# Register loads, bias sums, stores by position and early weight splits in a two-layer expert kernel

## The chip, the cores and the metric

The kernel runs on one core of one Trainium2 chip. The metric is the device time of one execution in microseconds (us), the median of several runs. A profile of one further execution shows each engine: TensorE (PE, its weight loads PEld), VectorE (DVE), ScalarE (ACT), GpSimd (POOL) and SyncE (SP, which only issues transfers here).

## The reference

The input x has 32 sequences of 128 tokens with 512 features (4096 tokens). Two layers follow each other; each adds a residual.

```python
# layer 0, condition: a shared expert and 2 of 8 routed experts for each token
shared = (silu(x @ sw1.T) * (x @ sw3.T)) @ sw2.T              # 512 -> 1024 -> 512
s = sigmoid(x @ router_w.T + cond @ router_t_w.T)             # the second term: one row per sequence
_, idx = top_k(s + router_bias, 2); gates = s[idx] / sum(s[idx])
routed = sum over both of gates * (gelu(x @ rw1[e].T) @ rw2[e].T)   # 512 -> 256 -> 512
h = (shared + routed) / 3
# layer 0, feed-forward: each sequence picks one of 8 experts from its last token
sel = argmax(softmax(gelu(h_last @ Wp1 + bp1) @ Wp2 + bp2))
x = x + h + 0.3 * ((gelu(h @ W1[sel] + b1) @ W2[sel] + b2) @ Wo + bo)
# layer 1, condition: tokens mixed with their predecessor, 16 experts chosen by token id
xk, xr = x + (prev - x) * maa_k, x + (prev - x) * maa_r
slot = place of the token in its expert's list, up to 256 tokens each, else dropped
y = square(relu(expert_in @ w_key)) @ w_value, gathered back by slot
z = sigmoid(xr @ w_recept) * y
# layer 1, feed-forward: a recurrence over 32 steps with gates f, i, c, and an output tanh
c = sigmoid(f) * c + sigmoid(i) * tanh(g) ; h = tanh(z @ wo.T + c @ uo.T + bo) ; x = x + h
```

## The kernel before, in words

A float32 product is made of three matmuls: `split` (L64, L65) cuts each operand into a high part (an ACT cast) and a low part (a DVE subtraction that waits for the cast), and `mm3` (L82) adds high times high, high times low and low times high. So every operand goes through ACT and DVE before TensorE may use it. A scheduler orders the instructions of each engine by the program's order and its own costs; `tc.issue_after(x)` keeps an instruction behind x, and `behind(last_split)` keeps one behind both halves of a split. An engine works its queue in order.

The work runs in these stages; the times are those of the profiled execution.

1. 0 to 305 us: the shared expert for the first 16 sequences, in four groups of four sequences (`shared`, with `up` and `down` for each of eight columns). Between its matmuls `mid0` puts the router for all tokens (`router`, tiles xr, xrhl, rt) and `seq_bias` (tiles pr, ps_tb, tbias), the cond @ router_t_w term; the condition `n + w == 1` in `mid0` holds for two half-columns. Later `hook2` runs the steps of `choose` and `slots`, which sort tokens into blocks and slots on DVE, and loads the routed experts' weights. `fetch` puts raw loads on SP. The copies of expert biases into `bias_d` (L770) stand in the program after stage 2, but depend on nothing, and the scheduler put them at 3.6, 17.5 and 18.1 us on SP.
2. 305 to 547 us: routed blocks of 128 token rows of one expert. For each block, `turn_x` transposes gathered rows (ptx) and splits them into xb; `r_up` makes 12 matmuls (pur) against the expert's up weights and a gelu (ge); `turn_h` transposes the result (pth, split into hbr); `r_down` makes 6 matmuls (por) and stores the rows. In the order of TensorE's queue, block i's pur are followed by ptx of block i + 1, the six por of block i - 1 and pth of block i. The expert of a block is known only at run time: `first_col` loads its column offset into a TensorE register (L663, a queue instruction), and each pur and por has an instruction in front of it that computes its address from that register. There are 64 blocks that always run, and up to seven more that run in pairs under `tc.If` (`maybe`, L702), placed after every sixth block from block 16 on. `used` is their number, loaded by four engines.
3. 548 to 827 us: the shared expert for the other 16 sequences; between them `combine` (L793, L794) sums shared and routed output of finished sequences, which `get_o` fetches (o, shc, xc), and `policy` picks each sequence's expert and sorts sequences by expert, so that position p stands for sequence `seq_i[p]`.
4. 827 to 1431 us: the feed-forward of layer 0, one sequence at a time in that sorted order (`up`, `bend`, `down`, tiles pu, pt, hb, po). `combine` for the last four sequences and `policy` for the last eight (`late`) run between them. `close` ends a pair of sequences (pb, x1), `mix_r` forms xr, `send_k` transposes and stores xk rows to `xk_d` and `send_v` stores the receptance rows (pv) to `v_d`. Both stores go to the row of the sequence, `rows_of`, whose number an engine loads into a register (`seq`, L1048).
5. 1431 to 1810 us: the 16 experts of layer 1, each with eight pieces of weights of 512 KB (`fetch_piece`, `split_piece`: rawD, wD; `use_piece`: phD, poD). `fetch_rows` gathers an expert's rows from `xk_d` by `slot_t`, `turn_rows` transposes and splits them (ptD, xe). The results go to `res_d`.
6. 1810 to 2495 us: the recurrence; each step gathers y from `res_d` by `gat_i`, loads r from `v_d`, and multiplies (ptF, then gates ps_c, ps_i, ps_f, output poF).

Of the kernel before, what the change touches and what calls it, by code (L numbers as in the profile page):

```python
# [20 lines left out]
P = 128  # L21
# [28 lines left out]
def tile_kernel(ctx: ExitStack, tc: tile.TileContext, a: dict, out: bass.AP):  # L50
# [44 lines left out]
    bias_d = dram.tile([E0 * P, 3 * KD], F32, tag="bias", name="bias_d")  # L95
    v_d = dram.tile([N, D], F32, tag="v", name="v_d")
    sh_d = dram.tile([(NG // 2 + 1) * GT, D], F32, tag="sh", name="sh_d")
    o_d = dram.tile([NBLK * P, D], F32, tag="o", name="o_d")
    xk_d = dram.tile([N, D], F32, tag="xk", name="xk_d")
# [31 lines left out]
    seq_i = const.tile([P, NB], I32, name="seq_i")  # L131
    s0_i = const.tile([P, NB], U32, name="s0_i")
# [17 lines left out]
    pad = const.tile([P, 416 // 4], F32, name="pad")  # L150
# [7 lines left out]
    with ExitStack() as sa:  # L158
# [6 lines left out]
        def fetch(src, name):  # L165
            t = raw_p.tile([P, D], F32, tag="raw", name=name)
            nc.sync.dma_start(out=t, in_=src)
            return t

# [35 lines left out]
        def fetch_x(g):  # L205
            if g < NG:
                x_raw[g] = [fetch(a["x"][g][:, k, :], f"xraw_{g}_{k}") for k in range(KD)]
# [68 lines left out]
        with ExitStack() as s0:  # L276
# [32 lines left out]
            fetch_sw(1)  # L309
            ps_acc = s0.enter_context(tc.tile_pool(name="ps_acc0", bufs=4, space=PSUM, **kw))  # L310
# [51 lines left out]
            def seq_bias():  # L362

                ps = ps_r.tile([P, NB, E0], F32, tag="r", name="ps_tb")
                for k in range(KD):
                    pr = rtile([P, NB, E0], f"pr_{k}")
                    nc.vector.tensor_tensor(
                        pr,
                        condT[:, k, :].unsqueeze(2).to_broadcast([P, NB, E0]),
                        rtw[:, k, :].unsqueeze(1).to_broadcast([P, NB, E0]),  # L370
                        ALU.mult,
                    )
                    mm(ps, ones, pr, k == 0, k == KD - 1)
                nc.vector.tensor_copy(tbias, ps)
# [3 lines left out]
            def fetch_r(i):  # L378
                g, k = divmod(i, KD)
                if 0 < g < NG:  # L380
                    xrs[i] = fetch(a["x"][g][:, k, :], f"xr_{g}_{k}")
# [165 lines left out]
            def slots():  # L547
# [28 lines left out]
                yield from invert(slot_t, [hi], [lo], NSLOT // P, "st")  # L576
                zero = rtile([P, D], "zero")
# [15 lines left out]
            def cut(m):  # L593
                return min(NR, KD + (NR - KD) * (m - 1) // 15) if m > 0 else 0

            def mid0(n, w):

                if n < KF:
                    m = 2 * n + w
                    for i in range(cut(m), cut(m + 1)):  # L600
                        router(i)
                    for i in range(cut(m + 1), cut(m + 2)):
                        fetch_r(i)
                    if n + w == 1:
                        seq_bias()
# [3 lines left out]
            def hook2(g, c):  # L609

                if g == 0:
                    next(steps[0], None)
                    return
                if g == 1 or (g == 2 and c < 5):
# [40 lines left out]
        with s1:  # L655
# [9 lines left out]
            def r_up(i, e=None):  # L665
                if e is None:
                    with tc.issue_after(last_up[0]) if last_up else nullcontext():
                        e = first_col(i)
                x = xb.pop(i)
# [30 lines left out]
            def maybe(n):  # L700
                es = [first_col(i) for i in pairs[n]]
                with tc.If(used > pairs[n][0]):  # L702
                    for i, e in zip(pairs[n], es):
                        r_up(i, e)
# [8 lines left out]

            for i in range(NFULL + 1):
                if i < NFULL:
                    r_up(i)
                    if i + 1 < NFULL:
                        turn_x(i + 1, bx, "xb")
                    if i + 3 < NFULL:
                        take(i + 3)  # L720
                if i > 0:
                    stored = r_down(i - 1)
                if i < NFULL:
                    turn_h(i)
                n, step = divmod(i - FIRST, STEP)
                if i == FIRST - 4:
                    engines = (nc.tensor, nc.scalar, nc.vector, nc.sync)
                    used = nc.values_load(
                        used_i[0:1, 0:1], engines=[x.engine for x in engines], min_val=NFULL, max_val=NBLK
                    )  # L730
# [38 lines left out]
        for kind, i in BIAS.items():  # L769
            nc.sync.dma_start(out=bias_d[:, bass.ts(i, KD)], in_=a[kind][:, KD * D :])  # L770
# [42 lines left out]
        def policy(b0, b1, sm, ps_t, room=None):  # L813
# [69 lines left out]
            nc.vector.tensor_scalar(idxw[:, b0:b1], srow, part_f, None, ALU.add)  # L883
            seq = stile([P, nb], "seq")
            by_place(seq, num)
            nc.vector.tensor_copy(seq_i[:, b0:b1], seq)
            for k in range(KD):
                by_place(condS[:, k, b0:b1], condT[:, k, b0:b1])

# [8 lines left out]
        raws, bcol, changed = {}, {}, {}  # L898
# [3 lines left out]
        def fetch_w(i):  # L902
            if i < len(todo):
                kind, b = order[todo[i]]
                raws[i] = wg.tile([P, WROW], F32, tag="raw", name=f"rawB_{i}")
                nc.gpsimd.indirect_dma_start(
# [3 lines left out]
                )  # L910
                if kind == "W1a":
# [94 lines left out]

    with ExitStack() as sb:
# [35 lines left out]
        seqs, end_p = {}, None  # L1043

        def seq(p, queue=nc.sync):

            if (p, queue) not in seqs:
                seqs[p, queue] = queue.value_load(  # L1048
                    seq_i[0:1, p : p + 1], min_val=0, max_val=PARTS[where(p)[0]] - 1
                )  # L1050
            return seqs[p, queue]

        def rows_of(t, p, queue=nc.sync):

            return t[bass.ds((seq(p, queue) + where(p)[0] * PARTS[0]) * P, P), :]
# [5 lines left out]
        def fetch_hid(b):  # L1061
            if b < NB:
                hid_raw[b] = lp.tile([P, KD, P], F32, tag="hid", name=f"hidB_{b}")
                nc.sync.dma_start(out=hid_raw[b].rearrange("p k q -> p (k q)"), in_=by_seq(hid_d, b))
# [65 lines left out]
        def close(c, last=False):  # L1130
# [38 lines left out]
            for j in range(PB):  # L1169
                part = where(c * PB + j)[0]  # L1170
                nc.sync.dma_start(
                    out=x1_d[bass.ds(seq(c * PB + j) + part * PARTS[0], 1)].rearrange("o p k q -> (o p) k q"),
                    in_=x1[:, :, j, 1:],
                )
            xks[c] = xk, dx, x1
            return done, mixed

# [14 lines left out]
        def send_k(b, queue=nc.sync):  # L1192
# [6 lines left out]
            return queue.dma_start(out=rows_of(xk_d, b, queue), in_=rows).ins  # L1199

        def send_v(b):
# [6 lines left out]
            nc.sync.dma_start(out=rows_of(v_d, b), in_=r)  # L1208
# [12 lines left out]
        for b in range(-1, NB + 1):  # L1221
            c, j = divmod(b - 1, PB)
            if b + 1 < NB:
# [3 lines left out]
                fetch_hid(b + 3)  # L1227
            gated = b - 4 if b % 2 == 0 and 0 <= b - 4 < NB - 6 else None
# [11 lines left out]

            late, step = divmod(b - 3, 3)
            if 0 <= late < GB and step == 0:
                get_o(NB - GB + late, cb, 1)
            if 0 <= late < GB and step == 2:
                combine(NB - GB + late, ps_t)
            if late == GB and step == 2:
                policy(PARTS[0], NB, cb, ps_t)
            if b + 1 < NB:
                bend(b + 1, "a")

# [37 lines left out]
        with tc.issue_after(k_done), tc.issue_after(rows_done):  # L1288
            for b in range(NB - 4, NB - 2):
                send_v(b)  # L1290
            mix_r(NB // PB - 1, rTp, "rT")
            for b in range(NB - 2, NB):
                send_v(b)

    sf = ctx.enter_context(ExitStack())
    sw_.close()
    with ExitStack() as sd:
        kw = dict(reuse_waits="tile")  # L1300
        R = dict(side="right", **kw)
        first_p = sf.enter_context(tc.tile_pool(name="first_p", bufs=1, **kw))
        swb = sd.enter_context(ExitStack())
        ewb = swb.enter_context(tc.tile_pool(name="ewb", bufs=4, **kw))
        er = sd.enter_context(tc.tile_pool(name="er", bufs=6, **R))
        ex = sd.enter_context(tc.tile_pool(name="ex", bufs=2, **R))
        ewa = sd.enter_context(tc.tile_pool(name="ewa", bufs=8, **R))
        ep = sd.enter_context(tc.tile_pool(name="ep", bufs=2, **R))
        tq = sd.enter_context(tc.tile_pool(name="tq", bufs=3, **R))
        ps_h = sd.enter_context(tc.tile_pool(name="ps_hD", bufs=3, space=PSUM, **kw))  # L1310
        ps_t = sd.enter_context(tc.tile_pool(name="ps_tD", bufs=2, space=PSUM, **kw))
        ps_o = sd.enter_context(tc.tile_pool(name="ps_oD", bufs=3, space=PSUM, **kw))
# [4 lines left out]
        def fetch_piece(p):  # L1317
            if p < NPC:
                e, i = divmod(p, 8)
                raws[p] = er.tile([P, 1024], F32, tag="raw", name=f"rawD_{p}")  # L1320
                nc.sync.dma_start(out=raws[p], in_=a["w_key"][e, i] if i < 4 else a["w_value"][e, i - 4])

        def split_piece(p):
            if p < NPC:
                raw = raws.pop(p)
                ew = ewb if p % 12 >= 8 and p < NPC - 8 else ewa
# [12 lines left out]

        def turn_rows(e):  # L1340
# [45 lines left out]
        AHEAD, RAW = 8, 6  # L1386
        fetch_rows(0)
        for p in range(RAW):
            fetch_piece(p)
        turn_rows(0)  # L1390
        fetch_rows(1)
        for p in range(AHEAD):
            after = r_done if p < 4 else (k_done, rows_done)
            with tc.issue_after(after[0]), tc.issue_after(after[1]):
                split_piece(p)
            fetch_piece(p + RAW)
        for p in range(NPC):
# [14 lines left out]
            if p == NPC - 9:  # L1412
                swb.close()
                uci = sf.enter_context(tc.tile_pool(name="uci", bufs=1, **kw))
                uc, first_part = {}, {}

                def weight(name, pool, stage, bufs, tag="raw", parts=2, queue=nc.sync, pair=None):
# [5 lines left out]
                    for h in range(parts):  # L1423
                        raw = stage.tile([P, w], F32, tag=tag, bufs=bufs, name=f"raw_{name}{h}")
                        s = bass.ts(h, w)
                        queue.dma_start(out=raw, in_=flat[:, s])
# [8 lines left out]
    with sf:  # L1435
# [17 lines left out]
        def get_y(b):  # L1453
# [7 lines left out]
            nc.sync.dma_start(out=r, in_=v_d[b * P : (b + 1) * P, :])  # L1461
# [136 lines left out]
        for t in range(NB):  # L1598
            cT = cT_next
            v = {}  # L1600
            if t == 0:
# [3 lines left out]
                with tc.issue_after(z_done):  # L1605
# [178 lines left out]
```

## Time and profile before

| | us |
|---|---|
| median of 3 runs (2495.82 to 2498.42) | 2498.41 |
| profiled execution, its own time | 2497.22 |
| its span, first to last instruction | 2495.5 |
| TensorE busy in it | 2434.5 |
| DVE, ACT, POOL busy | 1326.8, 1034.5, 412.3 |
| mean granted TensorE clock | 0.991 |

The profile names an instruction by engine, line and tiles ("PE pur L82": a matmul that writes pur). A row of waits says which instruction waited for which, with the total, the count and the longest. A row of a timeline gives start, duration, and, in brackets, idle time before it and what ended that. "PEldq" and "PEq" are TensorE's instruction queue: register loads, branches, semaphore waits. "x31" is a count. In a table of stretches each engine has its busy time and, in brackets, its number of instructions; then come the granted clock, the share of the transfers and GB/s.

### The profile page before, as it was taken

The numbers are of one execution on the slowest core, as the hardware profiler recorded it, in microseconds if no ns is written. First come the engines' busy times: TensorE is split into PE (matmuls) and PEld (weight loads), VectorE is DVE, ScalarE is ACT, GpSimd is POOL, SyncE is SP. The second block draws the span as 40 slices with busy tenths as digits, with TensorE's granted clock in tenths as the row PEclk, the third lists the DMA queues.
The fourth block names the chain that finished last, engine by engine and source line by source line (L and its number), as shares of the span: only waits on it lengthen the run. The fifth ranks groups of instructions, "written<-read, shape, count | busy, mean of one in ns | idle before, by whom it ended". The sixth has DMA issues, their size and how long they took to land.

```text
span 2495.5 us, 36566 instructions
## 1 busy us (share of the span) xinstructions
PE 2434.5 (98%) x12932; PEld 2060.7 (83%) x12932; DVE 1326.8 (53%) x2265; ACT 1034.5 (41%) x1826; POOL 412.3 (17%) x462
## 2 busy tenths in 40 slices
PE   8999999999999899999999999999999999999996
PEld 5788888888888788888888889999978888888885
DVE  7897644456567344454454486766642333333336
ACT  4444533343224454454454376666532222222214
POOL 1000022221233233322222100000010000000003
PEclk9999999999999999999999999999999999999998
DMA  5545544457564333341342487777431111111017
GB/s 181 168 126 169 187 161 161 163 185 238 183 215 165 115 120 127 102 153 57 118 146 94 152 295 232 222 228 234 155 125 39 38 40 42 43 42 38 26 70 280
DMA packets 193402, 351.62 MB, mean 141 GB/s; under 512 B 37504, under 2 KB 72368, under 8 KB 190144
## 3 DMA queue, kind: packets, MB, share of 16 engines
q1 hardware_dynamic: 142080, 246.51, 29.9%
q0 software_dynamic: 36448, 75.95, 10.3%
q10 hardware_dynamic: 14688, 26.75, 3.0%
q8 instruction: 108, 1.77, 0.3%
q14 instruction: 78, 0.64, 0.1%
HBM read 373.94 MB, written 88.65 MB: 185 GB/s over the span
## 4 chain that ended last, share of the span: by engine, by line
PE 49%; DVE 2%; DMA 1%; ACT 0%; issue 0%; POOL 0%; SPq 0%; POOLq 0%; DVEq 0%; ACTq 0%
PE phD L82 7%; PE ps_c L82 7%; PE ps_f L82 7%; PE ps_i L82 7%; PE poD L82 7%; PE poF L82 3%; PE po L82 3%; PE pb L82 2%; PE pv L82 1%; PE ptF L1481 1%; PE ptC L1488 1%; PE ptD L1348 0%; DMA v_d<-r 0%; DMA rawD<-in_w_value_dram 0%; PE ptB L1196 0%
## 5 line engine op out<-in xcount | busy, mean ns | idle before, releaser
L65 DVE TENSOR_TENSOR wD<-rawD,wD 128x1024 fp32r<-128x1024 f32 x128 | 156.4, 1229 | 80.8 <-ACT wD L64 80.7
L82 PE MATMUL p<-xhl,swu 128*128 128x512 f32 x768 | 188.7, 397 | 6.5 <-ACT xhl L64 6.5
L82 PE MATMUL phD<-xe,wD 128*128 128x256 f32 x1536 | 186.9, 282 | 2.0 <-DVE hf L1367 2.0
L82 PEld LDWEIGHTS phD<-xe,wD 128*128 128x128 f32 x1536 | 186.0, 190 | 3.3 <-issue 2.2
L82 PE MATMUL p<-xhl,kept_u 128*128 128x512 f32 x768 | 184.3, 394 | 0.7 <-DVE kept_u L65 0.7
L82 PE MATMUL poD<-wD,hD 128*128 128x512 f32 x768 | 181.3, 392 | 0.0
L82 PEld LDWEIGHTS p<-xhl,swu 128*128 128x128 f32 x768 | 144.6, 190 | 36.9 <-ACT xhl L64 6.5
L82 PEld LDWEIGHTS p<-xhl,kept_u 128*128 128x128 f32 x768 | 141.9, 188 | 30.0 <-DVE kept_u L65 1.1
L82 PEld LDWEIGHTS poD<-wD,hD 128*128 128x128 f32 x768 | 142.0, 188 | 28.4
L64 ACT CAST wD<-rawD 128x1024 fp32r<-128x1024 f32 x128 | 133.2, 1047 | 55.4 <-PE poD L82 50.1
L281 POOL DMA_INDIRECT xg<-in_x_rows_dram,blk_t x71 | 67.6, 952 | 454.9 <-PE ptx L291 246.4
L1456 POOL DMA_INDIRECT y<-res_d,gat_i x32 | 30.8, 962 | 573.6 <-DVE r L1476 492.1
L82 PE MATMUL pur<-r,xb 128*128 x792 | 111.5, 291 | 7.2 <-issue 4.2
L82 PE MATMUL por<-r,hbr 128*128 x396 | 108.0, 407 | 1.2 <-ACT hbr L64 1.2
L82 PEld LDWEIGHTS pur<-r,xb 128*128 128x128 f32 x792 | 99.7, 192 | 9.0 <-issue 6.9
L65 DVE TENSOR_TENSOR xb<-ptx,xb 128x512 fp32r<-128x512 f32 x68 | 47.0, 691 | 106.4 <-ACT xb L64 104.7
L82 PE MATMUL poF<-z,wo_hl 128*128 128x512 f32 x384 | 96.4, 399 | 0.0
L82 PE MATMUL ps_f<-wf_hl,z 128*128 128x512 f32 x384 | 96.2, 399 | 0.0
L82 PE MATMUL ps_c<-wc_hl,z 128*128 128x512 f32 x384 | 94.7, 396 | 0.7 <-ACT z L64 0.7
L82 PE MATMUL pb<-rT,Wo_hl 128*128 128x256 f32 x768 | 94.7, 281 | 0.3 <-DVE rT L65 0.2
L82 PE MATMUL acc<-swd,as 128*128 128x512 f32 x384 | 95.0, 392 | 0.0
L82 PE MATMUL pv<-w_recept_hl,xr 128*128 128x512 f32 x384 | 93.1, 391 | 0.5 <-ACTq L934 0.4
(1017 smaller groups left out, 4955.6 us busy)
## 6 DMA issues: line engine op xcount, KB each, us to landing
rawD<-in_w_key_dram SPq DMA_DIRECT2D x64, 512.0 KB, 4.3
rawD<-in_w_value_dram SPq DMA_DIRECT2D x64, 512.0 KB, 4.4
swr<-in_sw_dram SPq DMA_DIRECT2D x120, 256.0 KB, 3.2
o_d<-obr SPq DMA_DIRECT2D x66, 256.0 KB, 2.4
xraw<-in_x_dram SPq DMA_DIRECT2D x32, 256.0 KB, 4.2
rraw<-in_rw_dram SPq DMA_DIRECT2D x32, 256.0 KB, 3.0
xc<-in_x_dram SPq DMA_DIRECT2D x32, 256.0 KB, 3.5
hid_d<-o ACTq DMA_DIRECT2D x32, 256.0 KB, 2.2
```

Source lines behind the costliest of these rows:

```text
L64: first = nc.scalar.copy(hi, src).ins
L65: done = nc.vector.tensor_tensor(lo, src, hi.bitcast(F32), ALU.subtract).ins
L82: done = nc.tensor.matmul(ps, lhsT=left(hl, k), rhs=right(hr, k), start=start and k + n == 0, stop=stop and 3 * k + n == last,)
L281: nc.gpsimd.indirect_dma_start(out=xg[i], out_offset=None, in_=a["x_rows"], in_offset=bass.IndirectOffsetOnAxis(ap=blk_t[:, i : i + 1], ax ...
L1456: got = nc.gpsimd.indirect_dma_start(out=y, out_offset=None, in_=res_d, in_offset=bass.IndirectOffsetOnAxis(ap=gat_i[:, b : b + 1], axis=0),)
L1481: nc.tensor.transpose(pt[:, k, :], r[:, bass.ts(k, P)], ident)
L1488: nc.tensor.transpose(pt[:, k, :], c[:, bass.ts(k, P)], ident)
```

## The change

- Start: pieces 0 and 2 of the first group's x are loaded by ACT's queue. Router loads have their own six buffers and stay behind the first loads. `cut` begins the router two half-columns later. `seq_bias` sums its four products on DVE, makes one product on TensorE, and is called once, at the last column of group 0. The three copies into `bias_d` go to group 1's first columns, each behind the last load.
- Routed blocks: `know(i)` loads the register of a block, behind the last pur of the block before it. The registers of conditional blocks are loaded the same way, in the blocks before their branch; `used` is loaded behind a pur as well.
- Stage 4: `get_o`, `combine` and `policy` of the late sequences stand behind named loads and behind bend's split. xk and v rows are stored at the row of the position, without a register. `policy` notes `pos_i` and `moved` (how far a sequence's rows are shifted), and `by_position` corrects `slot_t` with it.
- Layer 1: the pools for raw pieces, rows and five weight pieces are opened early; the first pieces are fetched and five of them split before or amid the last gates of stage 4. One store to `x1_d` goes behind those loads.
- Recurrence: r is loaded from the row of the position, with a register load on SP for each sequence. One weight load is kept behind the last r load.
- The tile pad shrinks from 416 to 32 bytes for three new small tiles.

```diff
-        def fetch(src, name):
+        def fetch(src, name, queue=nc.sync):
...
+                x_raw[g] = [
+                    fetch(a["x"][g][:, k, :], f"xraw_{g}_{k}", nc.scalar if g == 0 and k % 2 == 0 else nc.sync)
+                    for k in range(KD)
+                ]
...
-                    mm(ps, ones, pr, k == 0, k == KD - 1)
+                    if k > 0:
+                        nc.vector.tensor_tensor(pr, pr, sum_, ALU.add)
+                    sum_ = pr
+                ps = ps_r.tile([P, NB, E0], F32, tag="r", name="ps_tb")
+                mm(ps, ones, sum_, True, True)
...
-                return min(NR, KD + (NR - KD) * (m - 1) // 15) if m > 0 else 0
+                return min(NR, KD + (NR - KD) * (m - 3) // 13) if m > 2 else 0
...
-                    if n + w == 1:
-                        seq_bias()
...
+                if g == 1 and c % 2 == 0 and c < 6:
+                    kind = list(BIAS)[c // 2]
+                    with tc.issue_after(last_load[0]):
+                        nc.sync.dma_start(out=bias_d[:, bass.ts(BIAS[kind], KD)], in_=a[kind][:, KD * D :])
...
-            def r_up(i, e=None):
-                if e is None:
+            cols = {}
+
+            def know(i):
+
+                if i < NBLK:
                     with tc.issue_after(last_up[0]) if last_up else nullcontext():
-                        e = first_col(i)
-                x = xb.pop(i)
+                        cols[i] = first_col(i)
+
+            def r_up(i):
+                x, e = xb.pop(i), cols.pop(i)
...
             def maybe(n):
-                es = [first_col(i) for i in pairs[n]]
                 with tc.If(used > pairs[n][0]):
...
+            know(0)
             for i in range(NFULL + 1):
+                n, step = divmod(i - FIRST, STEP)
                 if i < NFULL:
                     r_up(i)
                     if i + 1 < NFULL:
+                        with tc.issue_after(loads[0]) if i == FIRST - 3 else nullcontext():
+                            know(i + 1)
+
+                        if -3 <= i - FIRST and n + 1 < len(pairs) - 1 and step in (3, 4):
+                            for q in pairs[n + 1][step - 3 : step - 2]:
+                                know(q)
                         turn_x(i + 1, bx, "xb")
...
+        def by_position(pool):
+
+            n = D // NB
+            for s in (bass.ts(i, n) for i in range(NSLOT // P // n)):
+                room = pool.tile([P, D], F32, tag="o0", name="room_slot").rearrange("p (i b) -> p i b", b=NB)
+                nc.vector.tensor_tensor(
+                    room, slot_b[:, s].unsqueeze(2).to_broadcast([P, n, NB]),
+                    iota_b.unsqueeze(1).to_broadcast([P, n, NB]), ALU.is_equal,
+                )
+                nc.vector.tensor_tensor(room, room, moved.unsqueeze(1).to_broadcast([P, n, NB]), ALU.mult)
+                by = pool.tile([P, (NB - PARTS[0]) * E0], F32, tag="pol_pr", name="by_slot")[:, :n]
+                nc.vector.tensor_reduce(by, room, AX.X, ALU.add)
+                nc.vector.tensor_tensor(slot_t[:, s], slot_t[:, s], by, ALU.add)
...
-            return t[bass.ds((seq(p, queue) + where(p)[0] * PARTS[0]) * P, P), :]
+        def rows_of(t, p):
+            return t[p * P : (p + 1) * P, :]
...
-            if 0 <= late < GB and step == 2:
-                combine(NB - GB + late, ps_t)
-            if late == GB and step == 2:
-                policy(PARTS[0], NB, cb, ps_t)
             if b + 1 < NB:
                 bend(b + 1, "a")
+            with behind(last_split):
+                if 0 <= late < GB and step == 2:
+                    combine(NB - GB + late, ps_t)
+                if late == GB and step == 0:
+                    policy(PARTS[0], NB, cb, ps_t)
+                if late == GB and step == 2:
+                    by_position(cb)
...
+        for p in range(2):
+            with behind(r_done):
+                split_piece(p)
+            fetch_piece(p + RAW)
+        with tc.issue_after(last_piece[0]):
+            store_x1(NB // PB - 1, 1)
+        with tc.issue_after(k_done), tc.issue_after(rows_done):
+            for b in range(NB - 4, NB - 2):
+                send_v(b)
+            mix_r(NB // PB - 1, rTp, "rT")
+            xr_done = last_split[1]
+            for b in range(NB - 2, NB):
+                send_v(b)
+        for p in range(2, FIRST):
+            with behind((r_done[0], xr_done)):
+                split_piece(p)
+            fetch_piece(p + RAW)
...
-            nc.sync.dma_start(out=r, in_=v_d[b * P : (b + 1) * P, :])
+            part, _ = divmod(b, PARTS[0])
+            with tc.issue_after(last_r[0]):
+                at = nc.sync.value_load(pos_i[0:1, b : b + 1], min_val=0, max_val=PARTS[part] - 1)
+            last_r[:] = [nc.sync.dma_start(out=r, in_=v_d[bass.ds((at + part * PARTS[0]) * P, P), :]).ins]
```

## The prediction

> **What bounds the kernel now.** First the page's busy times, its forty slices and the chain that ended last:
>
> ```profile
> PE 2434.5 (98%) x12932; PEld 2060.7 (83%) x12932; DVE 1326.8 (53%) x2265; ACT 1034.5 (41%) x1826; POOL 412.3 (17%) x462
> ...
> PE   8999999999999899999999999999999999999996
> ...
> PE 49%; DVE 2%; DMA 1%; ACT 0%; issue 0%; POOL 0%; SPq 0%; POOLq 0%; DVEq 0%; ACTq 0%
> ```
>
> TensorE sets the time almost everywhere: idle in it costs its full length, idle elsewhere nothing until TensorE waits for it. So I read TensorE's waits next, longest first; the last number is the longest single wait, in us:
>
> ```profile
> PE po L82 <- DVE hb_0a L65: 6.7, 1, 6.7
> PE p L82 <- ACT xhl L64: 6.5, 1, 6.5
> PE pur L82 <- issue: 4.2, 1, 4.2
> PE ptD L1348 <- DMA rowsD<-xk_d,slot_t: 2.4, 2, 1.4
> PE ptF L1481 <- DVE r L1476: 2.3, 1, 2.3
> PE phD L82 <- DVE hf L1367: 2.0, 1, 2.0
> PE pur L82 <- PEq L702: 1.9, 1, 1.9
> PE rt L56 <- DVE rwa L359: 1.8, 1, 1.8
> PE ps_tb L56 <- ACT zt L397: 1.7, 1, 1.7
> ```
>
> About 30 us, nearly all at places that the change touches. Last, the routed blocks, where the change moves register loads: busy time in four stretches (ahead of the first branch, around it, on to the second, around that), then the second block's start, then what a register load occupies in TensorE's queue.
>
> ```profile
> 311.00:364.00 53.00, 52.90 (x369) 48.09 (x368) 26.75 (x46) 21.30 (x48) 15.58 (x18) 1.00 0.56 184
> 364.00:374.00 10.00, 5.77 (x29) 5.36 (x28) 1.74 (x3) 0.81 (x3) 0.65 (x1) 0.66 0.16 53
> ```
> ```profile
> 310.57 1.11 PE L82 MATMUL por<-r,hbr 128*128 x4
> 311.51 0.38 PE L682 MATMUL pth<-ident,ge 128*128 128x128 f32 x2
> 311.99 1.26 PE L82 MATMUL pur<-r,xb 128*128 x8
> ```
> ```profile
> L663 PEldq TENSOR_LOAD <-blk_e x1: 307/307/307, 311.2 to 311.2; - x1
> ```
> ```profile
> L291 PE MATMUL ptx<-ident,xg x4: 270/272/272, 341.2 to 341.6; 128*128 128x128 f32 x4
> L291 PEldq EVENT_SEMAPHORE  x1: 51/51/51, 340.9 to 340.9; - x1
> ```
>
> A normal block has no idle time: 52.90 of 53.00 us are busy, at full granted clock. A block takes 3.44 us: 12 pur at 0.117 us start to start, 6 por at 0.231, 4 ptx and 2 pth at 0.108.
>
> **The register loads in the blocks.** A load is three queue instructions; from its start to the next instruction of the queue is 0.69 us (the shorter cases; median 0.72). While TensorE still has matmuls handed over to it, that is hidden. Before, 56 of the loads stand behind the pth transposes: six por of 0.231 us are queued ahead and cover the load. The one case without that cover is shown above: the load starts at 311.20, the next pur runs at 311.99, so 0.79 us from load to matmul on an empty array; pth to pur is 0.37 us instead of 0.11, and one more 0.10 is lost behind it.
>
> After, the built order has 63 places with loads, and all but the first block's stand directly behind the twelfth pur and ahead of ptx (in one case por): 56 single, 6 double, 1 triple with the used count. How far is the queue ahead there? The third pur waits for DVE's xb low half, which ends 0.34 us before that pur runs, in every block; so the queue can be ahead no more than that, and pur at 0.117 us builds up no lead. The last fence shows it: the wait in front of ptx is handled at 340.9 and ptx runs at 341.2 (0.34 us), of which about 0.1 is the shortest possible. I read 0.2 us of true lead on 62 blocks (0.18 median, 0.23 mean). With the load in between, ptx runs 0.69 − 0.2 = about 0.5 us later. Nothing regains it: ptx starts the chain ACT xb (0.59), DVE xb (0.69), third pur, which moves along, and the por behind ptx keep their time. 63 × 0.5 = 31.5; the 8 further loads of the double and triple places have no cover, 8 × 0.69 = 5.5. Cost **+37**. Bounds: 0, if the queue runs further ahead than I read; 63 × 0.79 + 5.5 = 55, if no lead remains.
>
> [...]
>
> What the old places cost goes away. Eight loads bunch ahead of the first branch, three ahead of the second: idle 4.40 and 2.08 us above the normal distance, then 24 pur at 0.213 instead of 0.117 (2.3 us; granted clock 0.66 in that stretch), and 0.37 for the case above. Sum 9.2, less about 0.4 for each of these two branches, which stay: **−8** (−6 to −9).
>
> **The start.** x pieces 0 and 2 are issued by ACT as its first instructions, not by SP behind others: first matmul at about 5.9 instead of 6.46, −0.6 (−0.8 to 0). The router begins two half-columns later, so rwa, ready at 18.3, is there: −1.8. The sequence bias was computed twice (its condition holds for two half-columns): 16 matmuls of 0.22 us and waits of 1.66 and 0.81. Now there is one call, products summed on DVE (three additions of some 0.4 us, DVE has room at that point), 2 matmuls: −3.1 and −2.4. Bias copies leave SP's start and go behind group 1's loads, 4 us each, covered by weights fetched two columns ahead; without that cover a copy delays one split by up to 4 us. Sum **−7.5** (−4 to −8.5).
>
> **After the second shared half (837 us).** The 6.7 us wait: DVE stood 10.0 us at L793, combine of the first late block, ahead of hb_0a in its queue, for shc, which landed at 841.6. Behind it the pace was halved for 2.1 us. After, combine, policy and by_position stand behind bend's split, and hb_0a comes first: **−8.5** (−7 to −9). by_position adds six DVE instructions of about 0.7 us beside a TensorE that is busy; hidden, else 4.
>
> **Into layer 1 (1410–1453 us).** The waits for rowsD, two of 1.05 and 1.39 plus ACT's 2.4 us wait between its two xk_d stores, come from stores with a run-time row: each waits for the one before. Rows are now fixed, so the gather starts about 3 us earlier. Five weight pieces are split ahead of or amid the last gates (ACT 1.05, DVE 1.23 each), which removes the phD wait of 2.0 and some 2 us of half pace, but can push the rows copies on ACT back by up to 1.5. Of some 9 us lost there, **−6** (−8 to −2).
>
> **The rest at about nothing.** slot_b, pos_i and moved are small DVE steps beside busy TensorE (a us each, uncovered). Layer 1's r loads each get a register load on SP: 0.26 + 0.15 us and its check, 32 of them, with SP waiting 521 us in that stretch for ptF; if late, ptF waits 0.7 us once. The wait of 2.3 us at 1818 hangs on the last res_d stores and stays. Taken as 0 (−2 to +2).
>
> **Sum** against the profiled execution: its span is 2495.5, its time 2497.22, so 1.7 lies around the span. −8 −7.5 −8.5 −6 +37 = +7: 2504.2. The median of the runs, 2498.41, is 1.2 above it: **2505**.
>
> **Rivals.**
> 1. *The loads are hidden* (20%). For it: 56 loads cost nothing before, and the queue may run ahead further than its start times tell. Against it: the block at 311 us, and the 0.34 us. Only the gains are left: 2498.4 − 30 = 2468, faster. The deciding point is near: the gains of 30 are used up when the stall is (30 − 5.5) / 63 = 0.39 us in place of 0.5.
> 2. *Half hidden* (7%): ACT, which ends ge just as ptx ends (341.885 and 341.84), gets room when ptx comes later, xb is earlier and the lead grows to 0.45. 63 × 0.24 + 5.5 = 21: 2489, faster.
> 3. *Worse than the stall* (13%). With no lead at all +55 gives 2523. [...] Each block would have 0.5 us of idle in 3.9. The row: idle of 1.9 us at 399 us was followed by a granted clock of 1.00, 4.2 us was not. [...]
> 4. *The gains don't come* (inside the range of the main case): the waits at 837 and 1436 us turn into others; with half of them, 2512.
>
> **How the numbers follow.** Main case 60%: 2505, its own range 2496 to 2514. Measurement tells about 0.2%, 5 us, from no change: 2493.4 to 2503.4 is "same". Of the main case about 3 points of the 60 fall below, 22 within and 35 above; rivals 1 and 2 give 27 to faster, rival 3 gives 13 to slower: 0.30, 0.22, 0.48. The range must take in rival 1's middle and the main case's upper end: 2466 to 2514 leaves out about 5 in 100 below and 15 above.
>
> **What would show it.** Right: a block period of about 3.95 us; gaps of 0.4 to 0.6 us from pur to ptx; no bunch of idle at the first two branches; hb_0a without a wait; ptD's waits shorter; rt and ps_tb gone from the list. Wrong: busy time near 100% in the blocks with the loads behind pur, which would make it 2468; or a granted clock below 0.9 there.

## The result: 2528 us, slower by 1.2%

| | before | changed |
|---|---|---|
| median, us (4 runs each) | 2498.41 | 2528.14 |
| lowest to highest | 2495.82 to 2499.13 | 2523.5 to 2533.92 |
| profiled execution, span | 2495.5 | 2521.8 |
| TensorE busy | 2434.5 | 2437.3 |

The ratio of the times is 1.0122, 95% interval 1.0097 to 1.0147. The direction was the forecast one and the largest term of the sum was right; the size, +30 us instead of +7, was not. Busy time and chain of the page:

```profile
PE 2437.3 (97%) x12918; PEld 2054.4 (81%) x12918; DVE 1331.1 (53%) x2283; ACT 1037.2 (41%) x1826; POOL 414.5 (16%) x462
...
PE 48%; DMA 2%; DVE 1%; ACT 0%; issue 0%; POOL 0%; SPq 0%; POOLq 0%; DVEq 0%; ACTq 0%
```

TensorE does the same work as before (2437 us) in a span that is 26 us longer. So its waits tell the rest; this is the view of waits of the changed kernel, TensorE alone:

```profile
PE ptx L300 <- PE pur L82: 19.0, 48, 0.7
PE ptx L300 <- issue: 10.3, 11, 1.5
PE p L82 <- ACT xhl L64: 6.6, 1, 6.6
PE pth L834 <- DVE o L831: 6.3, 4, 3.5
PE ptC L1568 <- DVE c L1596: 6.2, 1, 6.2
PE pv L82 <- DVE xr L65: 2.3, 1, 2.3
PE ptD L1429 <- DMA rowsD<-xk_d,slot_t: 2.2, 3, 1.7
```

Gone are po's wait for hb_0a (6.7), pur's bunch of loads (4.2 and 1.9), ps_tb's waits, and phD's wait for hf (2.0). New are 29 us ahead of ptx, which the prediction has, and three larger rows that it does not have: pth at L834 (combine), ptC and pv.

The first matmul of each tile marks off the stages. The same marks in both profiled executions, against the prediction's sum:

| stage, us | before | changed | measured | forecast |
|---|---|---|---|---|
| start, to the first pur | 305.4 | 296.1 | −9.4 | −7.5 |
| routed blocks, to the first matmul of the second shared half | 243.1 | 274.8 | +31.7 | +29 |
| second shared half, to sequence 2's bend | 312.2 | 304.2 | −8.0 | −8.5 |
| sequences 2 to 31 | 526.8 | 537.8 | +11.0 | 0 |
| last gates and layer 1's experts, to the first ptF | 433.0 | 427.0 | −6.0 | −6 |
| recurrence, to the last matmul | 652.8 | 659.8 | +7.0 | 0 |
| sum | | | +26.3 | +7 |

Two stages that the prediction put at nothing cost 18 us; the forecast and the measured sum are 19 apart.

The table has one profile of each kernel. The nine kernels of the experiments keep most stages as they are in one of these two, and so show how far a stage scatters. The start takes 296.6 to 301.3 us in eight of them that have the changed one, and 309.1 in one that has the old one: the gain is anything from 4 to 13 us. The last gates and layer 1 take 427.4 to 432.2 us in seven with the changed order, and 429.3 in one with the old one: −6.0 may be nothing. The two stages of 18 us stand clear of such scatter (experiments 4 to 6). (The profiled execution of the changed kernel is the fastest of its four, which is why +26.3 stands here and +29.7 in the medians.)

**The blocks.** In the timeline of TensorE each block has a gap ahead of ptx (start, duration, and in brackets the idle time); the table of two stretches, the second around the first branch, shows that the clock did not fall, and the last line, that of the load's source line, shows when the load starts:

```profile
315.73 0.73 PE L82 MATMUL pur<-r,xb 128*128 x5
316.87 0.63 PE L300 MATMUL ptx<-ident,xg 128*128 128x128 f32 x4 [0.41 <-PE pur L82]
317.25 1.65 PE L82 MATMUL por<-r,hbr 128*128 x6
318.74 0.38 PE L709 MATMUL pth<-ident,ge 128*128 128x128 f32 x2
318.88 1.63 PE L82 MATMUL pur<-r,xb 128*128 x12
320.88 0.63 PE L300 MATMUL ptx<-ident,xg 128*128 128x128 f32 x4 [0.37 <-PE pur L82]
```
```profile
316.00:364.00 48.00, 41.93 (x283) 36.51 (x282) 20.57 (x35) 16.40 (x37) 12.31 (x13) 1.00 0.46 153
364.00:374.00 10.00, 10.00 (x68) 8.89 (x66) 5.07 (x9) 3.31 (x8) 2.84 (x3) 1.00 0.35 106
```
```profile
L685 PEldq TENSOR_LOAD <-blk_e x1: 297/297/297, 316.1 to 316.1; - x1
```

A block takes 4.01 us from ptx to ptx here, 4.00 at the middle one, where it took 3.44. The load starts at 316.1 and ptx runs at 316.87. Measured from start to start and above the normal distance of 0.117 us, pur to ptx costs 39.0 us over 64 places, 0.54 at the middle one. The bunch at the first branch is gone: around it all of 10.00 us are busy, where 5.77 were before. Ahead of it 52.90 of 53.00 us were busy before, and now 13% of the stretch is idle.

### The profile page after: what moved, and what is told of

The parts are those of the page before. It is cut to its first block, busy times and chain, and to the rows that moved or that the text cites. A ratio compares the mean times of both kernels' runs of the same rounds, so it can differ in the third digit from the quotient of the medians.

```text
span 2521.8 us, 36589 instructions
## 1 busy us (share of the span) xinstructions
PE 2437.3 (97%) x12918; PEld 2054.4 (81%) x12918; DVE 1331.1 (53%) x2283; ACT 1037.2 (41%) x1826; POOL 414.5 (16%) x462
## 4 chain that ended last, share of the span: by engine, by line
PE 48%; DMA 2%; DVE 1%; ACT 0%; issue 0%; POOL 0%; SPq 0%; POOLq 0%; DVEq 0%; ACTq 0%
PE phD L82 7%; PE ps_f L82 7%; PE ps_c L82 7%; PE ps_i L82 7%; PE poD L82 7%; PE poF L82 3%; PE po L82 3%; PE pb L82 2%; PE pv L82 1%; PE ptC L1568 1%; PE ptF L1561 1%; PE ptD L1429 1%; DMA r<-v_d 0%; PE ptB L1254 0%; DMA rowsD<-xk_d,slot_t 0%
```

## The experiments

Stage times below are taken from each kernel's own profile with the marks of the table above.

**1. The loads moved behind pth, all else as changed.**

```diff
+                    turned[:] = [nc.tensor.transpose(pt[:, k, :], u[:, bass.ts(k, P)], ident).ins]
...
-                    with tc.issue_after(last_up[0]) if last_up else nullcontext():
+                    with tc.issue_after(turned[0]) if turned else nullcontext():
                         cols[i] = first_col(i)
...
                         turn_h(i)
+                    if i + 1 < NFULL:
+                        with tc.issue_after(loads[0]) if i == FIRST - 3 else nullcontext():
+                            know(i + 1)
...
```

The conditional blocks' loads, cut here, move along.

> The changed kernel with one thing moved: each block's register load stands behind the two pth transposes (where six por are queued ahead of it), not behind the twelfth pur; the conditional blocks' loads stay spread over the blocks. Theory, lead of the queue: the 39.0 us of excess between pur and ptx vanish, a block is 3.44 us again, the stretch from the first pur to the first matmul of the next shared half falls from 274.8 us to 235 to 239, the time to 2489 to 2492. Rival, the blocks slow down for another reason (gathers, clock after many small idles, address registers known too late): the stretch stays above 255 us and the time above 2508.

2499.02 us, ratio to before 0.9999 (0.9986 to 1.0011): 29 us of the loss are gone with this one move. The block stretch is 244.7 us, 30.0 less than in the changed kernel, and a stretch in its middle has no idle time:

```profile
304.00:346.00 42.00, 42.00 (x292) 38.23 (x293) 20.99 (x38) 16.85 (x38) 12.66 (x14) 1.00 0.55 178
```

It is not the 235 to 239 that I expected, and 1.6 more than in the kernel before. Four single loads that start at most 0.4 us ahead of the second pth, or behind it, still show 0.6 to 0.9 us from pth to pur; the one place with three loads shows 1.08; por and pth wait for ACT once each (1.1 us). Places with two loads show 0.4 at most, where 0.03 is normal. So behind pth nothing is left of the gain from spreading the conditional loads.

**2. The block part of the change alone, in the kernel before.** The diff is that of the change between `first_col` and the loading of `used`.

> The kernel before with the block part of the change alone: loads behind the twelfth pur, conditional blocks' loads spread, the used count behind a pur. Theory, short lead of the queue: 39 us of excess between pur and ptx, less the 9 us of the bunches at the first two branches: the block stretch from 243 to 273 to 276 us, time 2527 to 2530. Rival, the loss in the changed kernel needs something else of the change as well (other pools, other timing of the gathers): the stretch stays below 262 us and the time below 2516.

2530.3 us, ratio 1.0116 (1.01 to 1.0131). The stretch is 276.3 us, and pur to ptx has 38.4 us of excess. The loss needs nothing else of the change. Three rows of its waits; the last two matter further down, since this kernel is as before behind the blocks:

```profile
PE ptx L291 <- PE pur L82: 18.7, 48, 0.8
PE po L82 <- DVE hb_0a L65: 6.6, 1, 6.6
PE phD L82 <- ACT wD L64: 0.5, 1, 0.5
```

**3. Every load made twice, behind pur in the changed kernel and behind pth in that of experiment 1.**

```diff
+                nc.tensor.value_load(blk_e[0:1, i : i + 1], min_val=0, max_val=(E0 - 1) * RCOL)
                 return nc.tensor.value_load(blk_e[0:1, i : i + 1], min_val=0, max_val=(E0 - 1) * RCOL)
```

> The changed kernel with every block register load made twice, one behind the other, at its place behind the twelfth pur. Theory: no cover is left there, so each of the 71 added loads costs its whole 0.69 to 0.72 us: the stretch rises from 274.8 us by 49 to 51. Rival, part of the 0.54 us stall is something fixed (a restart of the array, a wait for the rows): an added load runs in its shadow and costs less than 0.4 us, the stretch rises by less than 30.

> The kernel with loads behind pth (stretch 244.7 us) with every load made twice there. Theory: the lead there is about 1.3 us from the load's start to the next pur; two loads and the restart take 1.48 us, so 0.15 to 0.25 us shows per single place and the whole of the added loads at the seven places that had two already: the stretch rises by 18 to 27 us, far less than the 49 to 51 of the same addition behind pur. Rival, a queue deep enough for all: less than 10 us; no cover at all: 49 or more.

Behind pur the stretch rises by 59.9 us to 334.6 (one execution, 2597.05 us); the excess of pur to ptx rises from 39.0 to 95.4, so an added load costs 0.79 us in the mean. Nothing of it is hidden, and it costs more than the 49 to 51 us expected: the second load of a pair takes longer there, 0.52 us where the first takes 0.30, and 0.90 to the next instruction of the queue where 0.69 is usual (medians). Why is open. Behind pth the same loads add 34.2 us (279.0; one execution, 2539.89 us), above the 18 to 27 expected but far below 49. Two timelines, the first with double loads behind pur, the second behind pth:

```profile
321.90 0.63 PE L300 MATMUL ptx<-ident,xg 128*128 128x128 f32 x4 [1.41 <-issue]
322.29 1.65 PE L82 MATMUL por<-r,hbr 128*128 x6
323.77 0.38 PE L710 MATMUL pth<-ident,ge 128*128 128x128 f32 x2
323.91 1.63 PE L82 MATMUL pur<-r,xb 128*128 x12
326.91 0.30 PE L300 MATMUL ptx<-ident,xg 128*128 128x128 f32 x1 [1.37 <-issue]
```
```profile
319.22 0.38 PE L710 MATMUL pth<-ident,ge 128*128 128x128 f32 x2
319.66 1.84 PE L82 MATMUL pur<-r,xb 128*128 x12
321.34 0.60 PE L300 MATMUL ptx<-ident,xg 128*128 128x128 f32 x4
```

Behind pth, two loads end about 0.3 us after the work queued ahead of them (pth to pur is 0.30 us at the middle place, where 0.03 is normal), and the twelve pur then run at the pace at which their address instructions follow each other, one in 0.124 us, not one in 0.117 (1.84 us for the twelve above instead of 1.63): that is the part that I had not counted, 8 of the 34 us. At both places the price of a load is about its length less the work queued ahead of it.

**4. wo not kept behind the last r.**

```diff
-                with tc.issue_after(z_done), tc.issue_after(last_r[0]):
+                with tc.issue_after(z_done):
                     wo1 = weight("wo", keep_p, yp, 2, "zo", KD)
```

> The changed kernel, but the weight wo of the recurrence is no longer kept behind the last r load. Theory: its four raw loads go out some 37 us earlier, its casts no longer stand ahead of step 0's forget gate on ACT, TensorE's wait of 6.2 us for ptC goes: 2521 to 2522. Rival, the r loads with their register loads on SP are what is late: the wait stays, 2528; or the raw loads push r back and ptF waits some 5 us in its place.

Why ptC waits 6.2 us in the changed kernel is seen on ACT:

```profile
1856.40 0.63 ACT L1589 ACTIVATE v_i<-v_i 128x512 f32<-128x512 f32 x1 [1.44 <-DVE v_i L1588]
1859.21 0.62 ACT L64 CAST wo_hl<-raw_wo 128x512 fp32r<-128x512 f32 x1 [2.18 <-DMA raw_wo<-in_wo_dram]
1859.74 0.63 ACT L1589 ACTIVATE v_f<-v_f 128x512 f32<-128x512 f32 x1
```

The forget gate v_f stands in ACT's queue behind a cast of wo, and that cast waits for its raw load. The four loads leave at 1843.8 to 1855.8, which is 3.9 to 15.9 us after the first ptF; in the kernel before they left between 14.6 us ahead of it and 9.7 us behind it. Without the pin the first leaves 12.2 us ahead of it again (16 us earlier, not the 37 that I had written), and the wait becomes:

```profile
PE ptC L1568 <- DVE c L1596: 2.9, 1, 2.9
```

The recurrence takes 654.8 us instead of 659.8, so 5.0 of the 7.0 us come from this pin. Five other profiles with the pin take 658.2 to 659.3; in the kernels of experiments 7 and 8, also without it, the stage takes 653.0 and 652.8, as before the change. The time, 2526.71 us, does not tell 5 us from the scatter of these runs; the verdict rests on the stage.

**5. combine ahead of bend again.**

```diff
+            if 0 <= late < GB and step == 2:
+                combine(NB - GB + late, ps_t)
             if b + 1 < NB:
                 bend(b + 1, "a")
             with behind(last_split):
-                if 0 <= late < GB and step == 2:
-                    combine(NB - GB + late, ps_t)
```

> The changed kernel, but the late combine stands ahead of bend again and not behind its split; its fetches stay pinned. Theory: pth no longer waits for a combine that stands behind a weight split on DVE; the four waits (3.66, 0.43, 0.48, 2.39 us and some half pace) go, about 7 us less: 2521. Rival, it was this order that removed the 6.7 us wait of the kernel before: the wait for hb comes back and the time stays or rises to 2530.

In the changed kernel DVE works in this order (L830 and L831 are combine):

```profile
945.64 0.69 DVE L65 TENSOR_TENSOR hb_6a<-hf_6a,hb_6a 128x512 fp32r<-128x512 f32 x1 [1.26 <-ACT hb_6a L64]
946.25 0.75 DVE L830 SCALAR_TENSOR_TENSOR o<-o,g,shc 128x512 f32<-128x512 f32 x1
946.91 2.35 DVE L65 TENSOR_TENSOR wB_W1b<-rawB,wB_W1b 128x1024 fp32r<-128x1024 f32 x2
949.18 0.48 DVE L1240 SCALAR_TENSOR_TENSOR dx<-dx,maa_r_sb,x 128x256 f32<-128x256 f32 x1
949.58 0.75 DVE L831 SCALAR_TENSOR_TENSOR o<-o,g,o 128x512 f32<-128x512 f32 x1
```

A weight split of 2.35 us and a dx step lie between combine's two instructions, and TensorE's pth waits for the second one, with the rest of po queued behind it: 3.5 us there, and the next transposes at half pace (four pth in 1.08 us, where four ptx take 0.63 in the blocks):

```profile
950.47 1.08 PE L834 MATMUL pth<-ident,o 128*128 128x128 f32 x4 [3.50 <-DVE o L831]
```

With combine ahead of bend, pth no longer waits for combine's DVE step in any of its four places; sequences 2 to 16 take 253.7 us as before, not 261.0: −7.3. (Five other profiles with the changed order take 262.7 to 264.0 there.) The next stage rises by 1.5; pv now waits 3.9 us, not 2.3, behind policy:

```profile
PE pv L82 <- DVE xr L65: 3.9, 1, 3.9
PE pt_0a L1150 <- ACT ue_0a L1143: 1.3, 1, 1.3
```

The time is 2523.8 us (ratio to before 1.0098). The rival fell: hb_0a's wait did not come back, so the order at bend was not needed to remove it. What stays is the pinned fetch in `get_o`: the first late load of shc leaves at 909.1 us there and at 904.0 in the changed kernel, but at 832.4 in the kernel before, so combine's DVE step no longer stands ahead of hb_0a. The pin was not undone alone.

**6. policy at its old step.**

```diff
-                if late == GB and step == 0:
+                if late == GB and step == 2:
                     policy(PARTS[0], NB, cb, ps_t)
```

> The changed kernel, but the second policy runs at the step where the kernel before ran it (sequence 17 instead of 15), with the slot correction behind it. Theory: at its new place the exp and its two table loads on ACT and some thirty small DVE steps stand ahead of xr's split, and pv waits 2.3 us and runs at half pace; at the old place they stand beside another kind of work, so about 5 us go: 2523. Rival, the same instructions cost the same one step later: 2528, the wait moves to another tile; or worse, since the slot correction then meets it.

In the changed kernel policy stands here, ahead of both halves of xr's split (L875 and L879 are policy):

```profile
1142.39 1.28 ACT L875 ACT_TABLE_LOAD   x1
1143.85 1.03 ACT L64 CAST xr<-dx 128x1024 fp32r<-128x1024 f32 x1
1148.14 0.20 DVE L879 RECIPROCAL rs<-su 128x8 f32<-128x8 f32 x1
1149.02 1.23 DVE L65 TENSOR_TENSOR xr<-dx,xr 128x1024 fp32r<-128x1024 f32 x1
1150.31 2.02 PE L82 MATMUL pv<-w_recept_hl,xr 128*128 128x512 f32 x6 [2.30 <-DVE xr L65]
```

In this run pv's wait for xr is gone, and sequences 16 to 24 take 147.7 us instead of 152.9 (149.1 before): −5.2. The whole kernel took 2525.23 us.

**7. Four things undone at once** (1, 4, 5 and 6).

> The changed kernel with four things undone at once: loads behind pth, combine ahead of bend, policy at its old step, wo not kept behind the last r. Theory, the four are separate places on TensorE: 29 (measured for the loads) + 6 + 5 + 5 us from the stage times give 2481 to 2484, faster than the kernel before by 14 to 17 us. Rival, the order at bend is what removed the 6.7 us wait, or policy and combine meet at sequence 17: the gain of one part is lost in another and the time stays at 2490 or more.

2480.89 us (2480.22 to 2485.14), ratio to before 0.9923 (0.991 to 0.9937): faster than both kernels. That is 47.3 under the changed kernel; the parts (29.1 for the loads; 7.3, 5.2 and 5.0 by their stages) add up to 46.6. Its longest waits:

```profile
PE p L82 <- ACT xhl L64: 6.1, 1, 6.1
PE ptD L1431 <- DMA rowsD<-xk_d,slot_t: 2.5, 3, 1.6
PE pur L82 <- ACT hbr L64: 2.3, 3, 0.9
PE rt L56 <- DVE rwa L369: 2.3, 1, 2.3
PE por L82 <- ACT hbr L64: 1.6, 2, 1.1
```

**8. In addition, layer 1's first splits behind the rows copies.**

```diff
-            with behind(r_done):
+            with behind((k_done, rows_done)):
                 split_piece(p)
...
-            with behind((r_done[0], xr_done)):
+            with behind((rows_done, xr_done)):
                 split_piece(p)
```

> The kernel with four things undone, and a fifth: layer 1's first five weight pieces are split behind the last rows copies again, not ahead of them; fixed rows and early fetches stay. Theory, the gain of 6 us between the last gates and the recurrence comes mostly from the fixed rows (shorter gather), the early splits give and take: the rows copies leave ACT up to 1.5 us earlier, ptD's waits of 1.6 us shrink, and phD finds its pieces 1 to 3 us late: 2480 to 2484, the stretch from the last bend to the first ptF within 2 us of 429.0. Rival, the early splits carry the gain: phD's wait of 2.0 us and its half pace come back and the stretch rises to 432 to 434, the time to 2484 to 2486.

2481.9 us (ratio to before 0.9943, 0.9927 to 0.996), no difference in the total that these runs tell. The first split starts 33.8 us behind the last bend, where it is 22.8 in the changed kernel and 46.8 in the kernel before, so this is halfway back. The stretch from the last bend to the first ptF is 432.7 us against 429.0: it rises into the rival's range, but the changed order alone takes up to 432.2, and not by the rival's wait. phD waits for nothing longer than 1.1 us; one ptD waits 5.5 us for its gathered rows:

```profile
PE ptD L1431 <- DMA rowsD<-xk_d,slot_t: 5.5, 1, 5.5
PE phD L82 <- ACT xe L64: 1.1, 1, 1.1
```

Why the rows land late there is open: two weight loads leave just ahead of the first gather (36.2 and 37.3 us behind the last bend, the gather at 37.7), but in experiment 7 weight loads leave among the gathers too (37.1, 39.0 and 41.8; gathers from 39.4 to 43.2). Early splits without fixed rows, and the parts of the start one by one, were not tried.

## Why the prediction went wrong

**Right, with its sizes.**

- The register loads: +37 forecast, 39.0 measured. The lead of the queue, 0.2 us at the twelfth pur and 1.3 us behind pth (in the kernel before, from the load's start to the next pur), fits experiments 1 to 3: the price follows the place.
- The bunches: −8 forecast; the excess from pth to pur and from pur to pur is 9.1 us smaller. (The prediction's reading of pth to pur, "0.37 us instead of 0.11", is off: the normal distance is 0.03. It moves the sum by 0.1.)
- The 837 us wait: −8.5 forecast. From sequence 0's first bend to sequence 2's it is 29.0 us before, 29.2 in experiment 2, and 20.4 in all nine profiles with the pinned fetch: −8.6.
- The start: −7.5 forecast, −9.4 measured, −4 to −13 over all profiles. One term is wrong: the first matmul starts at 6.06 to 6.63 us and not at 5.9 (6.46 and 5.72 without the change). ACT's first cast, which waits for the weight's load, begins at 5.40 instead of 3.63; that the x loads beside it delay it is likely, not tested. Nor did rt's wait for rwa go for good: it is 0.5 us here, and 2.1 to 2.6 in experiments 5 to 8.

**A match by luck.** Into layer 1, −6 and −6.0. I said that the gather starts 3 us earlier. It starts 39.1 us behind the last bend in the changed kernel and 39.2 in the kernel before: the two xk_d stores do leave together, but land 4.8 us later instead of 2.7 to 2.9, among weight loads. In this pair of profiles 5.4 of the 6.0 us lie behind the first phD, where phD's wait of 2.0 us and the half pace after it were (granted clock 0.50 from 1449.1 to 1452.4 us). But with the order of the kernel before, in experiment 2, phD waits 0.5 us and the stage takes 429.3 us, inside the 427.0 to 432.2 of the changed order. So the runs show no gain here that stands clear of the scatter.

**Wrong: what was put at nothing.** The two stages put at 0 cost 11.0 and 7.0 us, 18 of the 19 us by which the sum of the profiles was off. The step that failed in the first is the clause "combine, policy and by_position stand behind bend's split, and hb_0a comes first", whose gain I counted and whose cost I did not. To stand behind a split in program order does not make the two halves of combine neighbours: a weight split came between them, and TensorE's pth had been ordered ahead of the rest of po. That cost 7.3 us. Policy, two steps earlier, put small DVE steps and a table load on ACT ahead of xr's split: 5.2 us by experiment 6, 3.8 against the kernel before. I had priced by_position alone, as hidden, else 4, and for the others asked only what they no longer block, not who waits for them now. In the recurrence "The rest at about nothing" failed: I looked at the r loads and their register loads, whose wait is 1.2 us, and passed over the pin on wo in the same lines. It held the first of four loads back by 18 us against the rest of its stage, and their casts stand on ACT ahead of a gate: 5.0 of 7.0 us by experiment 4. The other 2 are not there in experiments 7 and 8; which of their edits removed them is open.

**The rivals.** Hidden loads: no. Half hidden: no, 0.54 us at the middle place and not 0.24. No lead at all: no, 39.0 us and not 55. A lower clock in the blocks, with 0.5 us of idle in each: no, 1.00 in a stretch that is 13% idle in gaps of 0.4 to 1.5 us. But a single idle of 3.5 us at 947 us was followed by a granted clock of 0.50 from 950.4 to 951.6 us and of 0.53 from there to 953.6, then 1.00. "The gains don't come" named the right kind of loss, waits that turn into others, at 837 and 1436 us; they came at 947, 1120 and 1148 us.

## What to carry to other kernels

In this kernel a register load on the engine that sets the time cost about its length less the work queued ahead of it (of 0.69 us, 0.54 showed at the middle place behind the twelfth pur; behind pth the middle of the blocks had no idle time): put it behind long instructions (here six por, 0.231 us from start to start), not behind short ones that follow a wait (here pur, 0.117 us). When a pin moves an instruction, ask of every engine which instruction now stands directly behind it and who waits for that; a pin that removes one wait can order a producer behind a weight split (2.35 us in experiment 5) or a late load (a wait of 2.18 us in experiment 4) elsewhere. A term of zero in the sum deserves the same look at the neighbours in the queue as the large terms.

## What I had not expected of the hardware

Stages in which the built order is the same differ between executions by steps that appear at one place and stay: against the changed kernel's own profile, +1.6 us between 100 and 110 us in five of the eight others with its start, and +1.7 to +3.7 us near 790 us in experiments 1, 4, 5, 6 and 7. So a change of 5 us is better read from its stage than from the total, and from more than one pair of profiles. Two register loads that follow each other directly in the queue start 0.69 us apart (median of 78) at both places; but the second took 0.52 us with TensorE idle behind pur and 0.30 behind pth, where por still ran.
